# Graph layer and attention layer on one core: projections as three float32r products instead of seven block products in float32

## The chip, the cores and the metric

The kernel runs on one core of a Trainium2 chip. The metric is device time in microseconds of the whole program, as the median of three runs. A core has these engines: TensorE (PE in the profile, PEld for its weight loads), VectorE (DVE), ScalarE (ACT), GpSimd (POOL) and SyncE (SP, which here only issues DMAs). Each takes its instructions in order, and they wait for each other through semaphores. DMAs are issued from the queue of an engine; an issue that must wait for a buffer keeps what stands behind it waiting too.

## What is computed

The input x holds 64 elements of 256 rows and 512 columns; adj is a symmetric 256 x 256 graph of zeros and ones. Two layers follow each other, each with a residual and a normalisation of the rows. Cut to what matters:

```python
# layer 0
mi = x @ Wi.T                                  # Wi, Wj: 512 x 512
mj = x @ Wj.T
out0 = deg * (mi + b) + adj @ mj
h = layernorm(x + out0)
# layer 1, 8 heads of 64
q, k, v = h @ Wq.T + bq, h @ Wk.T + bk, h @ Wv.T + bv
scores = where(adj == 0, -inf, q @ k.T / 8)    # per head
attn = softmax(scores)
ao = attn @ v
y = layernorm(h + ao @ Wo.T + bo)
```

All is float32. The projections are those with Wq, Wk, Wv and Wo.

## The kernel before, in words

The main program, `unshifted_path`, works on pairs of elements: 32 groups of two (`NB = 2`, `NG = 32`). `for g in range(NG - 1)` is the main loop. A pass of it holds the attention of group g, layer 0 of group g + 1, the output projection of group g and the q, k and v projections of group g + 1; the first group's layer 0 and projections stand ahead of the loop (the prologue), the last group's attention after it.

Layer 0 of an element is a Strassen-like scheme (`l0_steps`): seven block products `step1` to `step7` of two matmuls each, 128 x 128 by 128 x 512, plain float32 (tiles `po`, weights `w0`, sums of x in `xS` from `sum_x`). Banks are called x, w, y and z; partial results are `u1`, `u2`, `u3` (tag `lu`). The result for the neighbours, `mj`, is cut into `hi` and `lo`, both float32r, and `neighbours` multiplies them with the graph: eight float32r matmuls of 512 columns (tile `pa`). `take` adds that to the residual `xh` and forms statistics, `give` normalises. x comes in twice, as `xh` (rows) and, in 32-row blocks, as `xB`, which DVE's 32 x 32 transposition turns into `xT` (`turn_x`). h goes to DRAM and back the same way (`send_h`, tiles `h_cols` and `hB`), and DVE turns it (`turn_h`).

The projections are a Strassen-Winograd scheme over the pair of elements (`pair_steps`, `qkv_steps`, `o_steps`): a projection is seven block products, each of four matmuls of 256 columns, float32 (tile `st`). Their left sides are blocks of h or of the attention output and sums of such blocks (`hS`, `oS`, made by `left_steps` on DVE); their right sides are seven `factor` tiles of 256 KB a projection, three of them blocks of the weights and four of them sums (`make_factors`, once, in the prologue), loaded from DRAM for every group through a ring of nine buffers (`stream`, `bring`), on SP's queue.

Attention goes in eight steps w a group, two heads a step, two steps a slot. `scores` makes a score tile `ps` (two banks); DVE adds the mask (`pe`), ACT takes the exponential, POOL adds the two halves (`pk`). `values` multiplies with v (`pav`), and `divide_two` has ACT copy that to `aoT`, TensorE make the denominators (`den`), DVE invert them (`rden`) and DMAs spread the inverses over partitions (`spread`); `multiply` applies them on POOL. POOL also sums the inverses in `rtot`, for a check at the end.

The order on the engines is written by hand for matmuls and for whatever passes through `in_order`; other instructions are placed by the scheduler. The score tiles have two buffers of two banks (`ps_s`), values one bank (`ps_v`), everything else three banks (`ps_m`).

Of the kernel before, what the change touches and what calls it, by code (L numbers as in the profile page):

```python
# [8 lines left out]
F32 = mybir.dt.float32  # L9
# [215 lines left out]
def unshifted_path(ctx, tc, flag, x, adj, wiT, wjT, b0, wqT, bq, wkT, bk, wvT, bv, woT, bo, out):  # L225
# [27 lines left out]
    AHEAD = 8  # L253
# [6 lines left out]
    p4 = ctx.enter_context(tc.tile_pool(name="p4", bufs=4))  # L260
    p6 = ctx.enter_context(tc.tile_pool(name="p6", bufs=6))
    stream = ctx.enter_context(tc.tile_pool(name="stream", bufs=AHEAD + 1))
# [35 lines left out]
    def load_x(b):  # L298
        if b < B:
            xh[b] = p6.tile([P, NT, D], F32, tag="xh", name="xh")  # L300
            nc.sync.dma_start(out=xh[b], in_=x[b].rearrange("(t p) d -> p t d", p=P))

    b_bc = p4.tile([P, D], F32, tag="u", name="b_bc")
    xB, hB = {}, {}

    def load_xB(b):
        if b < B:
            xB[b] = p1.tile([P, N // R, P], F32, tag="xB", name="xB")
            for q in range(D // P):
                nc.sync.dma_start(out=xB[b][q * R:(q + 1) * R],  # L310
                                  in_=x[b][:, q * P:(q + 1) * P].rearrange("(r a) n -> r a n", r=R))

# [11 lines left out]
    xT, xS, hT, hS, qT, kT, vv, aoT, oS = ({} for _ in range(9))  # L324


    ident = const.tile([P, P], F32, name="ident")
# [6 lines left out]
    rtot = const.tile([P, N], F32, name="rtot")  # L334
    nc.gpsimd.memset(rtot, 0.0)
# [7 lines left out]
    aT = p3.tile([P, NT, N], F32, tag="pk", name="aT")  # L343
    deg = small.tile([P, NT], F32, tag="deg", name="deg")
# [16 lines left out]
    def check_graph():  # L361


        exact = p1.tile([P, NT, N], F32, tag="oS", name="exact")
        in_order(nc.vector.tensor_tensor(exact, aT, graph.bitcast(F32), ALU.not_equal))
        in_order(nc.vector.tensor_reduce(inexact, exact.rearrange("p t n -> p (t n)"), AX.X, ALU.max))
        in_order(nc.vector.tensor_scalar(maskT, aT, 0.0, MASK, ALU.is_equal, ALU.mult))
# [9 lines left out]
    def load_bias(b, name):  # L377
        t = const.tile([P, NC], F32, tag=name, name=name)
        nc.sync.dma_start(out=t, in_=b)
        d = const.tile([P, 2], F32, tag=name + "d", name=name + "d")  # L380
        return t, d

    bq_sb, bqd = load_bias(bq, "bq")
    bk_sb, bkd = load_bias(bk, "bk")

    def bias_steps():
        for t, d in ((bq_sb, bqd), (bk_sb, bkd)):
            in_order(nc.vector.tensor_sub(d, t[:, 2:4], t[:, 0:2]))

    bv_t = small.tile([P, NC], F32, tag="bvt", name="bv_t")  # L390
    with nc.allow_non_contiguous_dma(reason="512 numbers, once"):
        nc.sync.dma_start(out=bv_t, in_=bv.rearrange("r (c p) -> p (r c)", p=P))
# [3 lines left out]
    def blocks_of(w):  # L396
        return (w.rearrange("(h c p) (j o) -> p h c j o", h=2, p=P, j=2) if w is woT else
                w.rearrange("(p h c) (j o) -> p h c j o", h=2, p=P, j=2))

    sources = {}  # L400
    for name, w in (("wq", wqT), ("wk", wkT), ("wv", wvT), ("wo", woT)):
        src = blocks_of(w)
        sources[name] = {B11: src[:, 0, :, 0], B21: src[:, 1, :, 0], B22: src[:, 1, :, 1]}


    def load_raw(w, tag):
        raw = p1.tile([P, 2, 2, 2, H], F32, tag=tag, name="raw")
        nc.sync.dma_start(out=raw.rearrange("p h c j o -> p (h c) (j o)"),
                          in_=w.rearrange("(c p) o -> p c o" if w is woT else "(p c) o -> p c o", p=P))
        return raw  # L410

    def make_factors(w, name, raw):
        kept = dram.tile([4, P, 2, H], F32, tag=name, name=name)
        t1, t2, t3, t4 = (p4.tile([P, 2, H], F32, tag="u", name="t") for _ in range(4))
        b11, b12, b21, b22 = (raw[:, h, :, j, :] for h in range(2) for j in range(2))
        for n, (t, p, m) in enumerate(((t1, b12, b11), (t2, b22, t1), (t3, b22, b12), (t4, b21, t2))):
            in_order(nc.vector.tensor_sub(t, p, m))
            nc.sync.dma_start(out=kept[n], in_=t)
        sources[name].update({T1: kept[0], T2: kept[1], T3: kept[2], T4: kept[3]})

    spread = p3.tile([P, NC, P], F32, tag="pk", name="spread")
# [3 lines left out]

    def fold_value_bias(raw):

        pb = score_bank("pb")
        for c in range(NC):
            h, kc = divmod(c, 2)  # L430
            matmul(pb, spread[:, c], raw[:, h, kc].rearrange("p j o -> p (j o)"),
                   start=(c == 0), stop=(c == NC - 1))
        nc.vector.tensor_add(bo_bc, pb, bo_bc)
# [4 lines left out]
    def bring():  # L438
        if queue:
            name, n = queue.pop(0)  # L440
            f = stream.tile([P, 2, H], F32, tag="factor", name="factor")
            nc.sync.dma_start(out=f, in_=sources[name][n])
            coming.append(f)

    def next_factor():
        f = coming.pop(0)
        bring()
        return f


    def norm_stats(t, order=anywhere):
# [3 lines left out]
        nc.vector.bn_aggr(mv, st)  # L455
        ve = small.tile([P, 1], F32, tag="ve", name="ve")
        nc.vector.tensor_scalar(ve, mv[:, 1:2], EPS, None, ALU.add)
# [3 lines left out]
        nc.gpsimd.tensor_tensor(rstd, ve, mhalf, ALU.pow)  # L461
# [26 lines left out]
    def turn_x(b, tag="xT"):  # L488
        if b < B:
            xT[b] = p1.tile([P, NC, N], F32, tag=tag, name="xT")  # L490
            transposed(xT[b], xB.pop(b))
            load_xB(b + 1)
# [9 lines left out]
    def l0_steps(b, late=False):  # L502
        banks, k = {}, {}
        order = in_order if late else anywhere
# [19 lines left out]
        def split(t):  # L524
            nc.scalar.copy(k["hi"][:, t, :], k["mj"][:, t, :])
            nc.gpsimd.tensor_tensor(k["lo"][:, t, :], k["mj"][:, t, :], k["hi"][:, t, :].bitcast(F32),
                                    ALU.subtract)

        def step1():
            product("x", raw(0, 0), B11, True)  # L530
            nc.scalar.copy(keeper("u1"), banks["x"])

        def step2():
            product("w", raw(1, 1), T4, True)
            add_scaled(1, banks["w"])

        def step3():
            product("x", raw(0, 1), B21, False)
            add_scaled(0, banks["x"])

        def step4():
            product("y", xS[b]["S2"], T2, True)
            nc.vector.tensor_add(keeper("u2"), banks["y"], k["u1"])

        def step5():
            product("z", xS[b]["S1"], T1, True)
            k["mj"] = p1.tile([P, NT, D], F32, tag="mj", name="mj")
            nc.vector.tensor_copy(k["mj"][:, 1, :], banks["z"])

        def step6():  # L550
            product("y", xS[b]["S3"], T3, False)
            nc.vector.tensor_add(keeper("u3"), banks["y"], k["u1"])
            nc.gpsimd.tensor_tensor(k["mj"][:, 1, :], k["mj"][:, 1, :], k["u3"], ALU.add)

            k["hi"] = p1.tile([P, NT, D], F32R, tag="hi", name="hi")
            k["lo"] = p1.tile([P, NT, D], F32R, tag="lo", name="lo")
            split(1)
            if not late:
                add_scaled(1, k["u3"])

        def step7():
            product("z", xS[b]["S4"], B22, False)
            order(nc.vector.tensor_add(k["mj"][:, 0, :], banks["z"], k["u2"]))
            split(0)
# [3 lines left out]
        def neighbours():  # L568
            k["pa"] = score_banks("pa")
            for i in (1, 0):  # L570
                for n, (j, part) in enumerate((j, part) for j in (1, 0) for part in ("hi", "lo")):
# [3 lines left out]
        def take(t):  # L575
            r = xh[b][:, t, :]
            if late and t == 1:
                in_order(add_scaled(1, k["u3"]))
            in_order(nc.vector.tensor_add(r, k["pa"][:, t, :], r))
            stats[t] = norm_stats(r, in_order)  # L580

        def give(t):
# [3 lines left out]
        return [step1, step2, step3, step4, step5, step6, step7, neighbours, lambda: take(1), lambda: take(0),  # L586
                lambda: give(1), lambda: send_h(b, 1), lambda: give(0), lambda: send_h(b, 0)]
# [530 lines left out]
```

## Time and profile before

| | us |
|---|---|
| median of three runs | 3068.26 |
| lowest and highest | 3067.78, 3070.22 |
| the profiled execution's own time | 3068.79 |
| its span, first to last instruction | 3066.9 |

The profile is of one execution. Rows give a line of the kernel, an engine, an operation, the tiles as out<-in, the shape and the count, then the busy time and the mean length of one in ns. Matmuls overlap, and their ends are modelled, so the step from one start to the next is a better measure than the length. A float32 matmul leaves two records, a float32r matmul one. A few groups of operations that the text uses:

| operation | engine | mean ns of one |
|---|---|---|
| mask addition `pe<-ps,maskT` | DVE | 1195 |
| reciprocal `rden<-den` | DVE | 1752 |
| row statistics `st<-xh` | DVE | 688 |
| transposition `hT<-hB`, 1024 elements | DVE | 2163 |
| exponential `pe<-pe` | ACT | 1058 |
| cast `hi<-mj` | ACT | 617 |
| sum of halves `pk<-pe` | POOL | 1278 |
| multiplication `aoT<-aoT,spread` | POOL | 1279 |
| bias addition `xh<-xh,degb`, 1024 elements | POOL | 2385 |

### The profile page before, as it was taken

The numbers are of one execution on the slowest core, as the hardware profiler recorded it, in microseconds if no ns is written. First come the engines' busy times: TensorE is split into PE (matmuls) and PEld (weight loads), VectorE is DVE, ScalarE is ACT, GpSimd is POOL, SyncE is SP. The second block draws the span as 40 slices with busy tenths as digits, with TensorE's granted clock in tenths as the row PEclk, the third lists the DMA queues.
The fourth block names the chain that finished last, engine by engine and source line by source line (L and its number), as shares of the span: only waits on it lengthen the run. The fifth ranks groups of instructions, "written<-read, shape, count | busy, mean of one in ns | idle before, by whom it ended". The sixth has DMA issues, their size and how long they took to land. (4 is left out here: it accounts for less than half of the span.)

```text
span 3066.9 us, 46810 instructions
## 1 busy us (share of the span) xinstructions
PE 3036.6 (99%) x16646; PEld 2124.6 (69%) x16646; DVE 2178.3 (71%) x3298; ACT 974.1 (32%) x1861; POOL 1519.5 (50%) x1255
## 2 busy tenths in 40 slices
PE   7999999999999999999999999999999999999998
PEld 4667766677766777666776667776677766677665
DVE  6776677766777667777677777677766777767775
ACT  2323333323333333332233332333333333323332
POOL 2544545544545445464454554454544546445453
PEclk9999999999999999999999999999999999999999
DMA  7455544455444555345553445544455444555333
GB/s 255 123 151 159 169 121 136 132 161 166 144 125 127 159 170 155 116 133 154 161 168 119 126 145 160 167 134 134 127 158 170 151 121 128 159 161 166 120 111 96
DMA packets 410411, 447.54 MB, mean 146 GB/s; under 512 B 40896, under 2 KB 300224, under 8 KB 409792
## 3 DMA queue, kind: packets, MB, share of 16 engines
q1 hardware_dynamic: 410176, 444.50, 48.8%
q8 instruction: 136, 2.23, 0.3%
q14 instruction: 99, 0.81, 0.1%
HBM read 340.79 MB, written 70.25 MB: 134 GB/s over the span
## 5 line engine op out<-in xcount | busy, mean ns | idle before, releaser
L461 POOL TENSOR_TENSOR rstd<-ve,mhalf 128x1 f32<-128x1 f32 x256 | 140.5, 552 | 707.3 <-DVE below L459 707.3
L816 POOL TENSOR_TENSOR pk<-pe 128x512 f32<-128x512 f32 x256 | 323.1, 1278 | 322.2 <-ACT pe L813 322.2
L290 PE MATMUL po<-w,xS 128*128 128x512 f32 x1024 | 462.2, 599 | 0.7 <-DVE xS L478 0.7
L290 PE MATMUL st<-hS,factor 128*128 128x256 f32 x2048 | 453.2, 379 | 1.5 <-DVE u L689 1.2
L290 PEld LDWEIGHTS st<-hS,factor 128*128 128x128 f32 x2048 | 388.4, 190 | 56.3 <-DVE xh L744 1.7
L813 ACT ACTIVATE pe<-pe 128x1024 f32<-128x1024 f32 x256 | 270.8, 1058 | 364.4 <-DVE pe L809 364.4
L290 PE MATMUL po<-w,xT 128*128 128x512 f32 x768 | 352.1, 601 | 14.8 <-DVE xS L477 9.3
L290 PE MATMUL st<-hT,factor 128*128 128x256 f32 x1536 | 352.5, 379 | 0.7 <-ACT hT L626 0.7
L290 PEld LDWEIGHTS po<-w,xS 128*128 128x128 f32 x1024 | 189.6, 190 | 235.6 <-issue 206.3
L809 DVE TENSOR_TENSOR pe<-ps,maskT 128x1024 f32<-128x1024 f32 x256 | 298.0, 1195 | 35.4 <-PE ps L290 35.4
L290 PEld LDWEIGHTS st<-hT,factor 128*128 128x128 f32 x1536 | 291.9, 190 | 41.8 <-ACT hT L626 0.9
L886 DVE RECIPROCAL rden<-den 128x256 f32<-128x256 f32 x127 | 222.5, 1752 | 76.6 <-PE den L290 73.6
L290 PEld LDWEIGHTS po<-w,xT 128*128 128x128 f32 x768 | 144.2, 191 | 181.9 <-issue 162.8
L887 POOL TENSOR_TENSOR rtot<-rtot,rden 128x256 f32<-128x256 f32 x127 | 106.8, 841 | 320.1 <-DVE rden L886 320.1
L290 PE MATMUL ps<-qT,kT 64*128 64x256 f32 x2048 | 265.0, 393 | 0.0
L290 PE MATMUL pav<-pe,v_sb 128*32 128x256 f32 x4096 | 248.4, 382 | 1.9 <-ACT pe L813 1.9
L290 PEld LDWEIGHTS ps<-qT,kT 64*128 64x128 f32 x2048 | 184.5, 186 | 78.1 <-issue 38.6
L744 DVE TENSOR_TENSOR xh<-st,xh 128x512 f32<-128x512 f32 x186 | 144.5, 777 | 132.2 <-PE st L290 132.2
L290 PE MATMUL st<-factor,hS 128*128 128x256 f32 x1024 | 234.8, 382 | 0.0
L290 PEld LDWEIGHTS pav<-pe,v_sb 128*32 128x32 f32 x4096 | 119.8, 110 | 164.3 <-issue 95.4
L290 PE MATMUL st<-factor,oS 128*128 128x256 f32 x992 | 224.2, 379 | 0.0
L290 PEld LDWEIGHTS st<-factor,hS 128*128 128x128 f32 x1024 | 192.1, 190 | 35.2 <-issue 10.6
(115 smaller groups left out, 4648.2 us busy)
## 6 DMA issues: line engine op xcount, KB each, us to landing
xB<-in_x_dram SPq DMA_DIRECT2D x256, 128.0 KB, 3.9
xh<-in_x_dram SPq DMA_DIRECT2D x64, 512.0 KB, 4.2
factor<-wq SPq DMA_DIRECT2D x128, 256.0 KB, 4.2
factor<-wk SPq DMA_DIRECT2D x128, 256.0 KB, 2.8
factor<-wv SPq DMA_DIRECT2D x128, 256.0 KB, 2.6
spread<-rden SPq DMA_DIRECT2D x1016, 32.0 KB, 1.9
factor<-wo SPq DMA_DIRECT2D x124, 256.0 KB, 3.2
h_cols<-xh SPq DMA_DIRECT2D x124, 256.0 KB, 3.0
```

Of the source, the lines that this page charges most:

```text
L290: in_order(nc.tensor.matmul(*args, **kw))
L461: nc.gpsimd.tensor_tensor(rstd, ve, mhalf, ALU.pow)
L744: nc.vector.tensor_add(dst, src, dst)
L809: nc.vector.tensor_add(pe.rearrange("p j t q -> p j (t q)"), ps.rearrange("p j t q -> p j (t q)"), maskT.rearrange("p t q -> p (t q)").uns ...
L813: in_order(nc.scalar.activation(flat, flat, AF.Exp, scale=QSCALE, accum_out=etot[:, NB * g + i, pr:pr + 1]))
L816: nc.gpsimd.tensor_tensor(pk, pe[:, :, 0, :], pe[:, :, 1, :], ALU.add)
L886: nc.vector.reciprocal(rden, den)
L887: nc.gpsimd.tensor_tensor(rtot, rtot, rden, ALU.add)
```

## The change

The projections no longer use block products. Each operand is cut into a head and a low part, and a product takes three float32r passes: head by head, low part by lifted low part, and a difference by a difference, which are added up in two banks X and Y; the result is X times a constant plus Y. h becomes the three tiles `hA` (head), `hL` (low) and `hD` (difference), the attention output likewise in the buffers of q, k and v. Each weight tile has three planes, made in the prologue by `make` on ACT and DVE and kept in DRAM; a factor is now 768 KB, there are 16 a group (four a projection), in a ring of six, and they are loaded from ACT's queue.

With this come other edits: the sums `hS` and `oS` go; the `lo` part of `mj` moves from POOL to DVE; the sum of inverses moves from POOL's `rtot` addition to an accumulating copy on ACT; the pairing of partitions in `values` and `den` is changed so that inverses are spread by four DMAs of 64 partitions instead of eight of 32; layer 0 of the next group starts earlier (`step1` to `step4` of its first element run in the pass before); h is sent, fetched and turned in halves of 128 rows, the first element's in the fourth slot and beside the output projection; nearly every instruction is put in program order; `xh` has five buffers instead of six; the fold of v's bias into the output bias moves into the first pass of the loop.

```diff
-    AHEAD = 8
+    RING = 6
+    UP, DOWN, LIFT = 1 + 2.0 ** -12, 1 - 2.0 ** -13, 2.0 ** 12
...
-    p6 = ctx.enter_context(tc.tile_pool(name="p6", bufs=6))
-    stream = ctx.enter_context(tc.tile_pool(name="stream", bufs=AHEAD + 1))
+    p5 = ctx.enter_context(tc.tile_pool(name="p5", bufs=5))
+    stream = ctx.enter_context(tc.tile_pool(name="stream", bufs=RING))
...
     def bring():
         if queue:
-            name, n = queue.pop(0)
-            f = stream.tile([P, 2, H], F32, tag="factor", name="factor")
-            nc.sync.dma_start(out=f, in_=sources[name][n])
+            name, j, first = queue.pop(0)
+            f = stream.tile([P, 3, D], F32R, tag="factor", name="factor")
+            if first:
+                make(f, name, j)
+            else:
+                in_order(nc.scalar.dma_start(out=f.bitcast(F32), in_=kept[name][j]))
             coming.append(f)
...
+    def make(f, name, j):
+        head, lift, diff = (f[:, i, :].rearrange("p (c o) -> p c o", c=NC) for i in range(3))
+        low = p3.tile([P, NC, P], F32, tag="lu", name="low")
+        for cs, raw in pieces(name, j):
+            in_order(nc.scalar.activation(head[:, cs], raw, AF.Identity, scale=DOWN))
+            in_order(nc.vector.tensor_sub(low[:, cs], raw, head[:, cs].bitcast(F32)))
+            in_order(nc.scalar.activation(lift[:, cs], low[:, cs], AF.Identity, scale=LIFT))
+        in_order(nc.vector.scalar_tensor_tensor(diff, low, LIFT, head.bitcast(F32), ALU.mult, ALU.subtract))
+        nc.sync.dma_start(out=kept[name][j], in_=f.bitcast(F32))
...
-            nc.gpsimd.tensor_tensor(k["lo"][:, t, :], k["mj"][:, t, :], k["hi"][:, t, :].bitcast(F32),
-                                    ALU.subtract)
+        def lows(t):
+            in_order(nc.vector.tensor_tensor(k["lo"][:, t, :], k["mj"][:, t, :], k["hi"][:, t, :].bitcast(F32),
+                                             ALU.subtract))
...
+    def split_head(parts, src):
+        in_order(nc.scalar.activation(parts[0], src, AF.Identity, scale=DOWN))
+
+    def split_diff(parts, src):
+        in_order(nc.vector.scalar_tensor_tensor(parts[2], parts[0].bitcast(F32), UP, src, ALU.mult, ALU.subtract))
+
+    def split_low(parts, src, engine):
+        in_order(engine.tensor_tensor(parts[1], src, parts[0].bitcast(F32), ALU.subtract))
...
+    def cols_product(banks, parts, f):
+        X, Y = banks
+        head, low, diff = parts
+        f = f.rearrange("p k (c o) -> p k c o", c=NC)
+        for c in range(NC):
+            matmul(X, f[:, 0, c, :], head[:, c, :], start=(c == 0), stop=False, skip_group_check=True)
+        for c in range(NC):
+            matmul(Y, f[:, 2, c, :], diff[:, c, :], start=(c == 0), stop=(c == NC - 1), skip_group_check=True)
+        for c in range(NC):
+            matmul(X, f[:, 1, c, :], low[:, c, :], start=False, stop=(c == NC - 1), skip_group_check=True)
+
+    def qk_step(g, store, tag, bias, m, kind):
+        def run():
+            if m == 0:
+                store[g] = p1.tile([P, NC, NB * N], F32, tag=tag, name=tag)
+            X, Y = banks = pair(kind)
+            cols_product(banks, hP[g], coming.pop(0))
+            dst = store[g][:, m, :]
+            in_order(nc.scalar.activation(dst, X, AF.Identity, bias=bias[:, m:m + 1], scale=UP))
+            bring()
+            in_order(nc.vector.tensor_add(dst, Y, dst))
+        return run
...
-        nc.gpsimd.tensor_tensor(rtot, rtot, rden, ALU.add)
...
+        spread = p1.tile([P, 2, N], F32, tag="spread", name="spread")
+        for half in range(2):
+            for pp in range(2):
+                issuer = nc.scalar if last and pp else nc.sync
+                in_order(issuer.dma_start(out=spread[half * DH:(half + 1) * DH, pp, :],
+                                          in_=rden[pp * DH:(pp + 1) * DH, :]))
+        total(rden, total_out)
         products.append((dst, spread))
```

`v_pair` makes v for one element (24 matmuls, four factors shared by both halves of its rows), and `o_steps` has three parts: `one(0)` and `one(1)` for the first element's halves, `two` for the second element, in which the second element's h is turned as well. The last two slots and the projections of the loop now read:

```diff
+        values(g, 4)
+        values(g, 5)
+        multiply()
+        h11 = turn_h(b1, 1)
+        split_head(*h11)
+        split_low(*h11, nc.gpsimd)
+        divide_two(g, 5)
+        load_xB(b3 + 1)
+        now, later = scores(g, 6), scores(g, 7)
+        now()
+        low2()
+        head, diff = three(("qT", "kT"))
+        split_head([head[:, :, :N]], aoT[g][:, :, :N])
+        later()
+        split_diff(*h11)
+        if g + 2 < NG:
+            next_p[0][1]()
+        split_diff([head[:, :, :N], None, diff[:, :, :N]], aoT[g][:, :, :N])
+        nb2()
+        add2(1)
+        add2(0)
+        multiply()
+        aoP[g] = [head, None, diff]
+        split_head(*ao_parts(g, 1, upper))
+
+        values(g, 6)
+        values(g, 7)
+        aoP[g][1], = three(("v",))
+        split_low(*ao_parts(g, 0, every), nc.gpsimd)
+        stat2(1)
+        divide_two(g, 7)
+        split_low(*ao_parts(g, 1, upper), nc.gpsimd)
+        split_diff(*ao_parts(g, 1, upper))
+        if g + 2 < NG:
+            next_p[0][2]()
+        give2(1)
+        send_h(b2, 1)
+        stat2(0)
+        give2(0)
+        fetch_h(b2, 1)
+        send_h(b2, 0)
+        multiply()
+        h10 = turn_h(b1, 0)
+        split_head(*h10)
+        split_head(*ao_parts(g, 1, lower))
+        split_low(*ao_parts(g, 1, lower), nc.gpsimd)
+        split_low(*h10, nc.gpsimd)
+        fetch_h(b2, 0)
+        p, q = next_p, next_q
+        v, q_, k = projection_steps(g + 1)
+        end = finish_steps(g)
+        o = o_steps(g, "SMAS", lambda t: turn_h(b2, t))
+        o[0]()
+        split_diff(*h10)
+        split_diff(*ao_parts(g, 1, lower))
+        o[1]()
+        run([o[2], v[0]])
+        sum_x(b3)
+        v[1]()
+        turn_x(b3 + 1)
+        run([end[0], q_[0], end[1], k[0], end[2], q_[1], end[3], k[1]])
```

## Prediction

> **What bounds the kernel now.** I read the page's busy shares first, then the matmul timeline of one group of two batch elements, then busy times by stage, then single rows.
>
> ```profile
> PE 3036.6 (99%) x16646; PEld 2124.6 (69%) x16646; DVE 2178.3 (71%) x3298; ACT 974.1 (32%) x1861; POOL 1519.5 (50%) x1255
> ```
>
> PE has no idle time to give, so only its own work counts, until another engine is late. In the timeline (start, us, engine, line, out<-in) one group runs from one `st<-factor,aoT` to the next:
>
> ```profile
> 1555.32 1.99 PE L290 MATMUL st<-factor,aoT 128*128 128x256 f32 x8
> ...
> 1557.61 0.40 PE L290 MATMUL pa<-hi,graph 128*128 128x512 f32 x1
> ...
> 1558.78 0.40 PE L290 MATMUL pa<-lo,graph 128*128 128x512 f32 x1
> ...
> 1562.47 5.34 PE L290 MATMUL st<-hT,factor 128*128 128x256 f32 x24
> 1567.65 1.89 PE L290 MATMUL st<-factor,aoT 128*128 128x256 f32 x8
> ...
> 1649.71 1.99 PE L290 MATMUL st<-factor,aoT 128*128 128x256 f32 x8
> ```
>
> A period is 1649.71 - 1555.32 = 94.39 us; there are 31. A plain float32 record of 256 columns takes (1567.65 - 1562.47)/24 = 0.216 us, and a matmul is two records. The only float32r matmuls, `pa`, step by (1558.78 - 1557.61)/5 = 0.234 us at 512 columns, one record each.
>
> ```profile
> 1513.40:1555.30 41.90, 41.90 (x273) 20.79 (x271) 31.09 (x39) 14.23 (x26) 24.35 (x21) 1.00 0.24 69
> 1555.30:1607.80 52.50, 52.50 (x253) 45.60 (x250) 36.24 (x64) 16.10 (x33) 23.15 (x20) 1.00 0.70 206
> sum 94.40, PE 94.40 PEld 66.39 DVE 67.34 ACT 30.33 POOL 47.50; mean PE 47.20 PEld 33.20 DVE 33.67 ACT 15.17 POOL 23.75
> ```
>
> These are the attention stage and the projection stage. DVE has 67.3 us of work in 94.4, so it has room, but two rows show that it isn't free to use it:
>
> ```profile
> 1531.69 0.42 DVE L479 TENSOR_TENSOR xS<-xT 128x256 f32<-128x256 f32 x1
> 1532.03 1.50 DVE L480 TENSOR_TENSOR xS<-xT,xS 128x256 f32<-128x256 f32 x1
> ...
> 1531.76 2.90 POOL L526 TENSOR_TENSOR lo<-mj,hi 128x512 fp32r<-128x512 f32 x2 [0.73 <-ACT hi L525]
> ```
>
> The same subtraction takes 0.42 us, and 1.50 us beside a POOL operation.
>
> **What the Trainium skill says.** "FP8 and Floating Point Precision", TensorE Precision Notes: true float32 is four passes through the array. The trace agrees (512 columns as two records of 0.43 us). "TensorE: Matmul & The Clock Gate", Back-to-back issue gap: N/2.4 + 2.5 ns, 216 ns for 512 columns; the plain records agree, the float32r ones show 234, and the measurement decides. "SBUF — State Buffer", SBUF: two separate sides: DVE and GpSimd share a port pair under an exclusive lock, which a DVE operation with two SBUF inputs takes against a GpSimd operation that reads SBUF; the loser waits for the whole instruction. The 1.50 us row agrees.
>
> **The change part by part.**
>
> *Products.* Out go 4 projections x 7 products x 4 matmuls x 2 records = 224 records x 0.216 = 48.4 us a group. In come 4 x 16 x 3 = 192 float32r matmuls of 512 columns x 0.234 = 44.9. PE's floor falls by 3.5, to 90.9. Their cost isn't shown for weights that change at every matmul and for two banks in turn: 0.216 (the skill's gap) would give 3.4 more, 0.25 (as far above the measured value) would take 3.2. I take 0.234, whose weight loads are also repeated.
>
> *DVE.* Out: sums hS, oS (8 x 0.69), combination of q, k, v (10 x 0.69, 4 x 0.48), o (5 x 0.69, 1.22), copies mj (2 x 0.69), two 2.1 us turns: 24.6 us. In: Y added to q, k, v (12 x 0.69), X and Y of o (4 x 0.75, 4 x 0.69), four half turns (half of 2.1, an estimate), differences of h and ao (6 x 0.69, 1.2), lows of mj, formerly POOL's (4 x 0.69), mj (2 x 0.69): 27.8. So 70.5 us.
>
> *ACT* gains heads (7, at 0.62 like the cast `hi`, one double), totals of inverses (4 x 0.5) and 18 DMA issues, about +7 to 37 us. *POOL* loses `rtot`, `lo`, `mj` and the additions of u (18.9) and gains lows (10): 38.6 us.
>
> *Where DVE is late.* DVE now stands in program order almost throughout. From the second element's second product (w, `q[1]`) to the second v pair (`v[1]`), PE has 4 attention slots x 4.23 (1520.32 to 1524.55 in the timeline), 8 layer-0 products x 1.72, two `pa` x 1.87, 72 projection matmuls x 0.234 and some 0.5 of switching: 51.7 us. DVE has 6 mask additions x 1.15, 4 reciprocals x 1.68, 4 statistics x 1.08, one turn of 2.07, four of 1.06, 8.1 of layer-0 additions, 2.6 of neighbour additions, 1.95 of lows, 1.7 of x sums, 5.05 of differences and 5.4 of o: 47.0. Then `v[1]` needs the last h difference and the bank that o's last addition frees. Room: 4.5 us after 0.2 for the hand-over. POOL works 25 of these 51.7 us, and DVE has twelve places with two SBUF inputs. Laying both orders side by side I find waits of 1.2 (u3 scaled, behind pk 5), 1.2 (low of mj, behind a multiplication), 0.75 (difference of h, behind pk 6), 1.2 (difference of ao, behind pk 7), 0.4 and 1.0 (upper and lower ao differences, behind their lows), 0.5 and 0.8 (last two h differences), and 0.75 where a difference waits for ACT's head: 7.8 us. The added waits hold what follows them: behind the lower ao difference stand o's additions, two turns, and so `v[1]`. 7.8 - 4.5 = 3.3 us late. Bounds: 0 (no collision beyond the room) and about 7 (each collides at a full 1.28 us, 15 less the 4.5, less what PE's own waits for the exponentials cover). I take 3.3.
>
> *Late next.* In q and k each product's Y bank must be freed by ACT within the four X matmuls, 0.93 us. With normalisations in between I find slack of 0.1 to 0.4 us, and book 0.2. So stalls of 3.5 return what PE gained: period 94.4.
>
> *h through DRAM.* Halves of 256 KB, four sends and four fetches, on SP in order; a fetch waits 3.0 us for its send. The last half lands about 1 to 3 us before its turn. Nothing is booked; if late, it delays `v[1]` one for one. SP loses 28 factor issues and 18 of 32 spreads; factors go to ACT's queue, where each stands behind the eviction that frees it. `load_x` waits there for a store (five buffers, not six); the additions behind it have until the next group.
>
> *Bytes.* Factors go from 28 x 256 KB to 16 x 768 KB, and a group from 14.0 to 19.4 MB. q1 moved 444.5 MB in 48.8% of the span, 297 GB/s while busy: 65 us of 94, with six factors in the ring. Hidden.
>
> *Prologue.* All 16 factors are made by ACT (head), DVE (low), ACT (lift) in ACT's order, 0.62 + 0.69 + 0.62 plus hand-overs, 2.2 to 2.6 us each, some 38 us of ACT's time that the old weight sums, on DVE, didn't need. Before, products begin at 48.07 and the loop at 96.57. After, ACT has from 48 on 38 of making, 15 of evictions, norms and heads, 5 of waiting for the graph check on DVE; then 14 us of PE stand behind the last made factor: the loop begins near 120. Four products (6.9) are then done that were inside the loop, so compare with 103.5: +17. The bias fold (3.4) moves into the loop, +3.4. Together +21, bounds 8 and 30.
>
> *Sum.* 3066.9 + 21 + 31 x (94.4 - 94.39) = 3088 us of span. The profiled run took 3068.79 around its 3066.9, and the median is 3068.26: forecast 3090.
>
> **Rivals.** (a) Forecast: DVE's port waits eat PE's gain, 3075 to 3130. Chance 0.42. (b) Faster: the waits stay within the 4.5 us of room, because POOL has 9 us less to do and each blocked operation also spaces the next; stalls are about 1.3, period 92.2, 3090 - 31 x 2.2 = 3022. It decides at a period of 93.7, 21/31 = 0.7 below the present one: 2.8 us of stall. For it: in the present order PE shows almost no idle time although DVE meets the same lock; against it: DVE has 3 us more to do, in a fixed order. 0.38. (c) DVE is the bound from slot two on, collisions near the full price: period 97, 3171. 0.11. (d) Factor transfers arrive late, since 12.6 MB are wanted mostly in q and k: 2 us for each of the last three, 3090 + 31 x 6 = 3276. Against it: 206 GB/s now in that stage. 0.02. (e) Between, within 0.2% of before. 0.07. That it doesn't do what it says is out: in the changed program's order each projection has 4 x 12 such matmuls.
>
> **Chances.** 0.2% is about what this measurement can tell from no change. Slower 0.42 + 0.11 + 0.02 = 0.55, same 0.07, faster 0.38. Range: (b) spreads over 2975 to 3060 with the float32r bounds, (c) to 3220; leaving a tenth on each side, 2998 to 3180; the forecast's own is 3075 to 3130.
>
> **What would show it.** Right: float32r steps of 0.234; the loop beginning near 120; PE idle before `v[1]` and in the second o stage, ended by DVE; DVE rows of 512 elements stretched from 0.65 to 1.3 and more beside POOL; DVE above 75%. Wrong: periods near 92 (b), waits for `factor` DMAs (d), steps of 0.216.

## The result and the profile after

| | before | after |
|---|---|---|
| median of four runs (lowest to highest), us | 3069.24 (3067.78 to 3070.41) | 3344.83 (3342.89 to 3354.18) |
| profiled execution, us | 3068.79 | 3342.89 |
| its span, us | 3066.9 | 3341.1 |
| median period of a group, us | 94.39 | 102.37 |
| mean TensorE clock granted | 0.999 | 0.949 |

The time is 1.0904 times that of before (95% interval 1.0883 to 1.0925). The forecast of 3090 had the direction right; the size is far off, and 3344.83 lies above the range of 2998 to 3180. By the starts of the output projection's first matmul in the 31 passes of the loop, the 274.2 us of longer span are 30.2 ahead of the first output projection, 239.4 in the 30 periods after it (7.98 each) and 4.7 behind the last. So the question is the period.

The page of after: the busy shares, then two DMA queues (packets, MB, share of 16 engines). q10 is the queue of ACT with the factors, q1 that of SP.

```profile
PE 3000.3 (90%) x15638; PEld 1954.2 (58%) x15638; DVE 2365.8 (71%) x3477; ACT 1186.9 (36%) x2247; POOL 1335.9 (40%) x992
...
q10 hardware_dynamic: 75808, 391.02, 33.0%
q1 hardware_dynamic: 229584, 215.69, 21.7%
```

PE was 99% busy before and is 90% now. DVE is at 71% in both, so a bound by DVE's amount of work is out. The DMA engines are at 55% on average, which hides a stretch that turns out to matter.

A v pair is the 24 matmuls that make v for one element. PE's timeline of after around the change from the first v pair to the second (start, us, engine, line, tiles; in brackets the idle time ahead and who ended it):

```profile
1517.77 0.40 PE L290 MATMUL pxy<-factor,hL 128*128 128x512 f32 x1
1526.99 0.77 PE L290 MATMUL pxy<-factor,hA 128*128 128x512 f32 x1 [8.82 <-DVE xh L743]
1527.56 0.63 PE L290 MATMUL pxy<-factor,hD 128*128 128x512 f32 x1
...
1531.83 0.44 PE L290 MATMUL px<-factor,hL 128*128 128x512 f32 x1
1532.10 0.40 PE L290 MATMUL pxy<-factor,hA 128*128 128x512 f32 x1
```

Nearly all the lost time is in this one place, once a group: 8.73 us of idle time on average over the groups, and then matmuls that step by 0.43 us instead of 0.227. The 12 steps from 1526.99 to 1532.10 take 5.11 us where 2.72 would do, 2.4 more. With 0.56 us before a `factor,kT` matmul of the output projection and 0.21 before `factor,v`, that is 11.9 us a group. PE's own work is 90.3 us (it is measured below), and 90.3 + 11.9 = 102.2, where the period is 102.4.

The bracket names DVE's addition at L743, the second of the additions that put the output projection into `xh`. It is easy to stop here and blame DVE, as the prediction did. DVE's own timeline of after shows what DVE did before that addition:

```profile
1509.87 0.69 DVE L743 TENSOR_TENSOR xh<-py,xh 128x512 f32<-128x512 f32 x1
1513.67 1.12 DVE L496 STREAM_TRANSPOSE hF<-hB 128x512 f32<-128x512 f32 x1 [3.11 <-DMA hB<-h_cols]
1515.48 0.69 DVE L605 SCALAR_TENSOR_TENSOR hD<-hA,hF 128x512 fp32r<-128x512 f32 x1 [0.70 <-ACT hA L602]
1521.85 1.12 DVE L496 STREAM_TRANSPOSE hF<-hB 128x512 f32<-128x512 f32 x1 [5.67 <-DMA hB<-h_cols]
...
1524.14 1.38 DVE L605 SCALAR_TENSOR_TENSOR hD<-hA,hF 128x512 fp32r<-128x512 f32 x1
1525.44 0.68 DVE L739 SCALAR_TENSOR_TENSOR xh<-pxy,xh 128x512 f32<-128x512 f32 x1
1526.16 0.69 DVE L743 TENSOR_TENSOR xh<-pxy,xh 128x512 f32<-128x512 f32 x1
```

At 1510.5 DVE had nothing left that it could do; PE started the first v pair only at 1512.38. So DVE was 1.9 us ahead, and then it stood twice, 3.11 and 5.67 us, for the two halves of h to come back from DRAM (2.1 and 5.9 in the median of the groups). The last half landed 1521.85 - 1517.77 = 4.1 us after PE's last matmul had started. Another 5.0 us passed between that landing and the end of the addition at 1526.85, because DVE then has the transposition, two additions, the difference of this half and two more additions to do, in this order. 4.1 + 5.0 = 9.1 of the 9.2 us between the starts of the two matmuls. In these 5.0 us the difference of h takes 1.38 us, where the row of the other half takes 0.69: POOL works on the low part of the same half at that time, so some 0.7 us of the waits that the prediction counted do lie on the path.

Why did the half land so late? The timeline of after shows the DMA issues on SP's queue (L624 sends, L629 fetches):

```profile
1506.17 0.36 SPq L624 DMA_DIRECT2D h_cols<-xh  x1
1508.57 0.34 SPq L629 DMA_DIRECT2D hB<-h_cols  x1
1509.00 0.39 SPq L624 DMA_DIRECT2D h_cols<-xh  x1
1516.48 0.33 SPq L629 DMA_DIRECT2D hB<-h_cols  x1
```

ACT's queue of after, over the same time:

```profile
1508.22 1.69 ACTq L441 DMA_DIRECT2D factor<-wv  x2
...
1514.88 0.33 ACTq L441 DMA_DIRECT2D factor<-wq  x1
1515.30 0.39 ACTq L441 DMA_DIRECT2D factor<-wk  x1
```

The first send took 2.4 us (its fetch could be issued at 1508.57). The second took 1516.48 - 1509.00 = 7.5, and its fetch 1521.85 - 1516.48 = 5.4. In the median of the groups it is the same: 7.5 and 5.4 us. Beside them run four factor loads of 768 KB, which the output projection's third part releases as it uses up its own factors. The order on SP may have a share too: the second half of h was ready when ACT had normalised it, but its send stands behind the first half's fetch and went out 1.5 us later (median). No run puts both sends ahead of both fetches, so what that alone is worth is not known.

The windows of after, for the 14 us in which these transfers meet and the 8 us behind them (span of the window, its length, then the busy time of PE, PEld, DVE, ACT and POOL, and at the end the clock, the DMA engines' busy share and GB/s):

```profile
1508.00:1522.00 14.00, 10.17 (x43) 7.54 (x41) 4.48 (x7) 1.12 (x2) 4.85 (x3) 0.99 0.80 281
1522.00:1530.00 8.00, 3.01 (x7) 2.46 (x8) 7.40 (x12) 1.60 (x3) 1.26 (x1) 0.50 0.00 0
```

For 14 us the DMA engines move 281 GB/s at a busy share of 0.80. That is near the 297 GB/s that SP's queue reached while busy in the kernel before, but it is no ceiling: from 1517 to 1520, between the second send and the arrival of the last half, the same trace has 410 GB/s at a busy share of 1.0, nearly all of it factors. For the next 8 us the engines move nothing. An average over the group hides both. The two lines also show the clock: 0.99 in the first window, 0.50 in the second.

### The profile page after: what moved, and what is told of

It reads as the page before. It is cut to its first block, busy times and chain, and to the rows that moved or that the text cites. A ratio compares the mean times of both kernels' runs of the same rounds, so it can differ in the third digit from the quotient of the medians.

```text
span 3341.1 us, 42660 instructions
## 1 busy us (share of the span) xinstructions
PE 3000.3 (90%) x15638; PEld 1954.2 (58%) x15638; DVE 2365.8 (71%) x3477; ACT 1186.9 (36%) x2247; POOL 1335.9 (40%) x992
## 3 DMA queue, kind: packets, MB, share of 16 engines
q1 hardware_dynamic: 229584, 215.69, 21.7%
## 5 line engine op out<-in xcount | busy, mean ns | idle before, releaser
L290 PE MATMUL po<-w,xT 128*128 128x512 f32 x768 | 376.3, 613 | 13.5 <-DVE xS L488 8.4
L290 PE MATMUL pxy<-factor,hA 128*128 128x512 f32 x256 | 119.4, 466 | 272.1 <-DVE xh L743 269.0
L608 POOL TENSOR_TENSOR hL<-hF,hA 128x512 fp32r<-128x512 f32 x124 | 186.8, 1507 | 425.9 <-ACT hA L602 425.9
L496 DVE STREAM_TRANSPOSE hF<-hB 128x512 f32<-128x512 f32 x124 | 141.1, 1138 | 251.5 <-DMA hB<-h_cols 251.5
L373 POOL TENSOR_TENSOR xh<-xh,degb 128x1024 f32<-128x1024 f32 x64 | 152.5, 2383 | 291.2 <-issue 80.7
L697 DVE TENSOR_TENSOR kT<-py,kT 128x512 f32<-128x512 f32 x128 | 88.5, 691 | 253.1 <-ACT kT L695 253.1
L602 ACT ACTIVATE hA<-hF 128x512 fp32r<-128x512 f32 x124 | 77.7, 627 | 457.4 <-DVE hF L496 457.4
L290 PEld LDWEIGHTS pxy<-factor,hA 128*128 128x128 f32 x256 | 56.0, 219 | 296.7 <-issue 281.2
L478 ACT ACTIVATE xh<-xh,shift,rstd 128x512 f32<-128x512 f32 x256 | 208.8, 816 | 8.6
L854 POOL TENSOR_TENSOR aoT<-aoT,spread 128x512 f32<-128x512 f32 x127 | 206.1, 1623 | 11.7 <-DMA spread<-rden 10.6
```

What stands on the lines that cost most here:

```text
L290: in_order(nc.tensor.matmul(*args, **kw))
L373: in_order(nc.gpsimd.tensor_tensor(xh[b], xh[b], degb, ALU.add))
L478: order(nc.scalar.activation(t, t, AF.Identity, bias=shift, scale=rstd))
L496: in_order(nc.vector.transpose(dst.rearrange("p c (n a) -> p a c n", n=R), blocks.rearrange("p a (r c) -> p a c r", c=NC)))
L608: in_order(engine.tensor_tensor(parts[1], src, parts[0].bitcast(F32), ALU.subtract))
L697: in_order(nc.vector.tensor_add(dst, Y, dst))
```

## The experiments

Theory after the profile of the change (called the transfer theory): the halves of h are late because 768 KB loads share the DMA engines with them. Rivals: DVE is late, by waits at the port or by its order, as the prediction had it; or the clock's fall is the main cost. Eight kernels were run; all are versions of the changed kernel, and none leaves out a part of the computation.

**Filling the gap with matmuls.** The first v pair, which needs only the first element's h, is computed twice.

```diff
-            for c in range(NC):
+            for c in (range(NC) if last else [*range(NC), *range(NC)]):
```

> The first v pair's 24 matmuls run twice (the second time over the first, same result): 24 x 0.227 = 5.4 us of matmuls more in each of 31 groups. Theory of transfers (the second element's h halves come late, whatever TensorE does): the second v pair starts no later than now, the wait before it shrinks from 8.8 to about 3.3 us, the clock is not taken down, so the 12 matmuls behind the wait step by 0.227 instead of 0.43: 2.4 us a group less, about 3345 - 31 x 2.4 = 3270. Theory that VectorE is late because it follows TensorE: the wait moves with the extra work, 5.4 us a group more, 3510. If the slow matmuls behind the wait have another cause than the wait: unchanged, 3345.

Measured: 3316.09 us (3314.63 to 3320.97), 1.0805 of before (1.0787 to 1.0823), mean clock 0.983. PE's timeline of this kernel:

```profile
1510.16 0.47 PE L290 MATMUL pxy<-factor,hA 128*128 128x512 f32 x1 [2.72 <-DVE xh L743]
...
1511.70 0.63 PE L290 MATMUL pxy<-factor,hA 128*128 128x512 f32 x1
1512.13 0.63 PE L290 MATMUL pxy<-factor,hD 128*128 128x512 f32 x1
```

Twenty-four more matmuls a group, 5.4 us, cost nothing: the idle time fell from 8.73 to 3.24 us. So what PE waits for does not come later when PE has more to do. The gain, 29 us or 0.9 a group, is less than the 2.4 that slowed matmuls cost in the changed kernel, and the time lies 46 us above the forecast. The lines show why: after an idle time of only 2.72 us the step still rises to 0.43, 1.5 us later. Of 30 groups, 21 had such slow matmuls (1.7 us lost, in the median) and 9, with idle times of 2.0 to 3.3 us, lost 0.1.

The idle time alone does not tell the two kinds apart, but the trace's record of the granted clock does. The clock changes only at multiples of 3.41 us from its first change, in every run here. In the loop of this kernel it fell after each of the 21 stretches between two such moments in which PE had been busy for 0.40 of the time or less, and after none with 0.48 or more. So an idle time of 2.7 us that falls into one stretch costs the clock, and one of 3.3 us that two stretches share does not; and since the fall comes at the end of the stretch, PE may be at work again by then. The rival that the clock is the main cost does not fit: by the steps it takes 2.4 of the 11.9 us lost in the changed kernel.

**Factor loads behind the last half of h.** The output projection's third part keeps its four factors and asks for the next four only after ACT has taken the head of the last half.

```diff
-                        rows_of_product(banks[t], parts, NT + t, coming[0], c, which)
-                coming.pop(0)
-                bring()
+                        rows_of_product(banks[t], parts, NT + t, coming[c], c, which)
...
             h0 = turn(0)
             split_head(*h0)
+            for _ in range(NC):
+                coming.pop(0)
+                bring()
```

> The four factor loads that are issued within o's third part (two of wv, one of wq, one of wk) are issued only after the last half of h has been turned. Theory of transfers: the sends and fetches of the second element's h no longer share the DMA engines with 768 KB loads; the second send takes 2.3 us instead of 7.4 and the fetches 2.5 to 3 instead of 5; the last turn on VectorE starts about 6 us earlier. TensorE then waits in the first v pair for wv instead, for some 4 us: period 97 to 99, 3180 to 3240. Theory of VectorE's ports: the sends and fetches hardly change, the last turn moves by under 1 us, and the wait for wv comes on top: slower, above 3400.

Measured: 3234.36 us (3231.45 to 3237.53), 1.054 (1.0522 to 1.0558), period 98.89. First SP's issues in this kernel's timeline:

```profile
1559.57 0.39 SPq L624 DMA_DIRECT2D h_cols<-xh  x1
1562.82 0.33 SPq L629 DMA_DIRECT2D hB<-h_cols  x1
```

Then DVE's timeline of the same kernel, at the last transposition, which waits 1.00 us and not 5.67:

```profile
1565.54 1.14 DVE L496 STREAM_TRANSPOSE hF<-hB 128x512 f32<-128x512 f32 x1 [1.00 <-DMA hB<-h_cols]
```

And PE's, in the first v pair:

```profile
1570.97 0.79 PE L290 MATMUL px<-factor,hA 128*128 128x512 f32 x1 [4.83 <-DMA factor<-wv]
```

The second send now takes 3.3 us and its fetch 2.7, 6.0 together instead of 12.9, with the same instructions and the same bytes; only what stands beside them differs. That is the transfer theory's cause, shown by taking it away. The 110 us that it gives are not the whole price, since the wait has changed its name: PE now stands 4.65 us a group for the third factor of v, which was asked for at 1566.8, and the clock falls in this gap too.

**VectorE's order.** In the changed kernel the additions stand behind the transposition that waits. Here they go ahead of it.

```diff
             split_diff(*h1)
-            h0 = turn(0)
-            split_head(*h0)
-            split_low(*h0, nc.gpsimd)
             add_x(1, 0, banks[0])
             add_y(1, 0, banks[0])
-            split_diff(*h0)
             add_x(1, 1, banks[1])
             add_y(1, 1, banks[1])
+            h0 = turn(0)
+            split_head(*h0)
+            split_low(*h0, nc.gpsimd)
+            split_diff(*h0)
```

> The changed kernel with the four additions of the output projection's third part put ahead of the transposition of the last half of h in VectorE's order; nothing else. In the changed kernel they stand behind it, and the first matmul of the second v pair waits for the last of them, since it frees its bank. Transfer theory (the last half of h is late itself): the wait moves by a few matmuls, from the first to the fourth, which is the first to read that half, and VectorE has less to do after the landing, some 2 us: between 0 and 2.5 us a group less, 3265 to 3345. Rival (the wait is the place of the additions in VectorE's order, and h alone would be in time): most of the 8.7 us and of the slowed matmuls after it go, 10 us a group, 3035 to 3080.

Measured: 3252.91 us (3247.57 to 3256.62), 1.0597 (1.0579 to 1.0614), period 99.26. PE's timeline of this kernel:

```profile
1578.45 0.47 PE L290 MATMUL pxy<-factor,hA 128*128 128x512 f32 x1 [0.41 <-DVE xh L743]
...
1583.56 0.80 PE L290 MATMUL px<-factor,hA 128*128 128x512 f32 x1 [4.17 <-ACT hA L602]
```

DVE's, at the last transposition:

```profile
1581.72 1.13 DVE L496 STREAM_TRANSPOSE hF<-hB 128x512 f32<-128x512 f32 x1 [3.41 <-DMA hB<-h_cols]
```

The wait moved from the first to the fourth matmul, as the transfer theory said, but the time lies in neither band: the gain, 3.1 us a group, is above that theory's 2.5 and far below the rival's 10. After the landing 1.8 us pass until PE goes on (1581.72 to 1583.56), where in the changed kernel it was 5.0. So the order in DVE's list is a second cause, in series with the first. Taken away alone, it leaves more than half of the lost time.

**More work for VectorE.** The transposition of the first element's second half is made three times, 2.2 us more for DVE in the stretch in which the prediction had it late.

```diff
+        twice = hB[b1, 0]
         h10 = turn_h(b1, 0)
+        transposed(h10[1], twice)
+        transposed(h10[1], twice)
```

> The changed kernel with the transposition of the first element's second half made three times instead of once, directly after one another in the fourth slot: 2 x 1.1 = 2.2 us more of VectorE's time a group, inside the stretch in which the prediction had VectorE late. Transfer theory (VectorE had finished its list 1.9 us before TensorE ended the output projection and then waited for the halves of h): the wait before the first v pair stays set by the DMA, so between 0 and 0.5 us a group, 3345 to 3360, and the idle time of TensorE before that pair stays between 8 and 9 us. Prediction's theory (VectorE late through waits at the port, each further microsecond of its work delays the v pair one for one): 2.2 x 31 = 68 us more, 3413.

Measured: 3319.16 us (3317.22 to 3326.42), 1.0821 (1.0803 to 1.0839). PE's timeline of this kernel:

```profile
1510.52 0.50 PE L290 MATMUL py<-factor,kT 128*128 128x512 f32 x1 [1.84 <-DVE kT L605]
...
1525.12 0.77 PE L290 MATMUL pxy<-factor,hA 128*128 128x512 f32 x1 [6.33 <-DVE xh L743]
```

DVE's, with the transposition made three times and the one that waits:

```profile
1503.49 3.44 DVE L496 STREAM_TRANSPOSE hF<-hB 128x512 f32<-128x512 f32 x3
...
1519.97 1.12 DVE L496 STREAM_TRANSPOSE hF<-hB 128x512 f32<-128x512 f32 x1 [5.76 <-DMA hB<-h_cols]
```

(The wait that the expectation places before the first v pair is the one before the second.) More work made the kernel 26 us faster; both theories missed that, the DVE theory by 94 us. DVE's delay does reach PE, but earlier, in the output projection (1.85 us a group before `factor,kT` and 0.7 before `factor,qT`, instead of 0.56 together), and the later wait shrinks by more than that: the sum of the idle times is 8.5 us, after 9.5. In most groups PE only waits earlier and not longer, for the last half of h comes when it came before. Counted from the first matmul of the output projection, it lands after 21.7 us in the changed kernel, 21.7 with the gap filled, 21.6 with the additions first and 21.6 here, but after 14.6 with the factor loads moved (medians of the traces). Neither PE's work nor DVE's order or work moves it; the loads do. Most periods stay at 102.3; six fall to between 95 and just over 100, and in these six the last half lands after 17.7 to 20.3 us. That the small wait in the output projection spreads the factor loads there is an inference; it was not tried by itself.

**TensorE turns the second element's h.** Eight transpositions of 128 x 128 by TensorE, in the middle of the output projection's third part, replace two sends, two fetches and two of DVE's transpositions. The score tile that they write is used up by the first v pair. The low parts of this h are now made by DVE instead of POOL, and all of its cutting stands ahead of the additions, so both causes are taken away at once here.

```diff
-        send_h(b2, 1)
...
-        fetch_h(b2, 1)
-        send_h(b2, 0)
...
-        fetch_h(b2, 0)
...
+        both = score_banks("pt_h")
...
+        pts = {t: both[:, 1 - t, :].rearrange("p (c n) -> p c n", c=NC) for t in (1, 0)}
+        for t in (1, 0):
+            for c in range(NC):
+                transpose(pts[t][:, c, :], xh[b][:, t, :].rearrange("p (n c) -> p c n", c=NC)[:, c, :], ident)
+        for t in (1, 0):
...
+            split_three(cut_parts(hP[g], slice(0, NC), cols), pts[t], nc.vector)
```

> The second element's h is turned by TensorE (8 transpositions, about 1 us a group) into a free pair of banks within o's third part and cut from there; it no longer goes through DRAM. The first element's still does. Theory of transfers: the wait before the second v pair goes (8.7 us) and with it the slow clock (2.5 us), TensorE pays 1 us: period 102.4 - 10 = 92 to 93, total 3030 to 3060, under the kernel before. Theory of VectorE's ports: VectorE has two turns of 1.1 us less, but its port waits stay, so 3 us or more of wait before the second v pair remain: period 95 or more, 3115 or more.

Measured: 3042.21 us (3041.34 to 3042.62), 0.991 of before (0.9893 to 0.9926), period 92.63, clock 0.995. The busy shares on the page of this kernel:

```profile
PE 2961.1 (97%) x15886; PEld 1942.7 (64%) x15886; DVE 2311.2 (76%) x3477; ACT 1192.1 (39%) x2247; POOL 1238.1 (41%) x930
```

Its timeline of PE, from the transpositions to the bank that they used:

```profile
1569.03 1.12 PE L293 MATMUL pt_h<-ident,xh 128*128 128x128 f32 x8
1569.91 0.47 PE L290 MATMUL px<-factor,qT 128*128 128x512 f32 x1
...
1574.12 0.50 PE L290 MATMUL pt_h<-factor,hA 128*128 128x512 f32 x1 [0.55 <-DVE hL L608]
```

The eight transpositions cost PE 0.88 us, and the period is 9.7 us shorter. The second v pair has no wait any more, the clock no longer falls in the loop, and the change, with this one trip to DRAM taken out, is 0.9% faster than the kernel before. DVE is busy almost without a break from the fourth slot to the second v pair, with the same stretched rows beside POOL, and all that PE waits for it is the 0.85 us of the next experiment.

**The first v pair's order.** What was left was 0.85 us a group before the first matmul into the bank that had held the turned h. The next kernel takes one half of the rows first, so that this bank is needed later.

```diff
-            for c in range(NC):
-                for t in (1, 0):
+            for c, t in ([(c, t) for c in range(NC) for t in (1, 0)] if last
+                         else [(c, t) for t in (1, 0) for c in range(NC)]):
```

> The kernel in which TensorE turns the second element's h, with one more edit: the first v pair takes its 12 matmuls for one half of the rows and then the 12 for the other, instead of the two halves in turn, so that the bank which the turning used is needed after 12 matmuls (2.7 us) and not after 3. If the 0.85 us a group before that bank's first matmul is a wait for VectorE's reading of the turned h alone: all of it goes, 31 x 0.85 = 26 us less, 3016. If VectorE is late there as a whole (it is busy almost without a break from the fourth slot on), the wait moves to the second v pair's bank, and half of it or less goes: 3029 to 3042.

Measured: 3039.65 us (3036.05 to 3042.18), 0.9901 (0.9885 to 0.9918). That is 2.6 us below the run before, whose runs lie within 1.3 us and this kernel's within 6.1: no clear difference. It is in the band of the second expectation, but not by its reason. PE's timeline of this kernel:

```profile
1572.42 0.39 PE L290 MATMUL px<-factor,hL 128*128 128x512 f32 x1
1573.54 0.50 PE L290 MATMUL px<-factor,hA 128*128 128x512 f32 x1 [0.73 <-DMA factor<-wv]
```

The wait for DVE is gone, and a wait for the fourth factor, which this order needs after 9 matmuls, is there with the same 0.85 us on average.

**Making weight tiles one ahead.** In the prologue ACT made a head, waited for DVE's low part, and made the lifted low part. Now the next head is issued in between.

```diff
+            if first:
+                finish = make(f, name, j)
+            while pending:
+                pending.pop()()
+            if first:
+                pending.append(finish)
...
+        def finish():
+            for cs, _ in cuts:
+                in_order(nc.scalar.activation(lift[:, cs], low[:, cs], AF.Identity, scale=LIFT))
+            in_order(nc.vector.scalar_tensor_tensor(diff, low, LIFT, head.bitcast(F32), ALU.mult, ALU.subtract))
+            nc.sync.dma_start(out=kept[name][j], in_=f.bitcast(F32))
```

> As the run before, and in the prologue the head of the next weight tile is issued on ScalarE ahead of the lifted low part of the present one, so that ScalarE does not stand idle 0.76 us for VectorE between the two. If the making of the 16 tiles by ScalarE sets the prologue, as the prediction has it, some 0.76 us for each of the first six and a part of the later ten go: the loop begins 4 to 8 us before 122.7, and the time falls by as much. If the raw weights or TensorE's own waits for banks set it: less than 1 us.

Measured: 3031.31 us (3029.23 to 3031.87), 0.9875 (0.9859 to 0.9892), 8.3 us less than the run before. The loop's first work, the fold of v's bias, starts at 112.03 us, where it was 123.70: 11.7 us earlier, more than the 4 to 8 expected, of which the time keeps 8.3. So ACT's order set a part of the prologue.

**Both waits of the first v pair at once.** Three factors with one half of the rows, the same three with the other half, then the fourth with both.

```diff
-                         else [(c, t) for t in (1, 0) for c in range(NC)]):
+                         else [(c, t) for cs in ((0, 1, 2), (3,)) for t in (1, 0) for c in cs]):
```

> As the run before, but the first v pair takes its matmuls in another order: three weight tiles with one half of the rows, the same three with the other half, then the fourth tile with both. The bank that held the turned h is then needed after 9 matmuls (2.0 us) instead of 3 or 12, the fourth weight tile after 18 (4.1 us) instead of 9. If the 0.85 us a group of both earlier orders were two separate waits of that size, one for VectorE's reading of the bank and one for the landing of the fourth tile, both are covered: 31 x 0.85 = 26 us less, 3005. If VectorE or the transfers are late as a whole, the wait turns up again further on (the second v pair), and the time stays between 3020 and 3032.

Measured: 2996.11 us (2994.09 to 2997.27), 0.9757 of before (0.9744 to 0.977), 35 us less than the run before; period 91.41. The busy shares on the page of this kernel:

```profile
PE 2945.1 (98%) x15886; PEld 1941.8 (65%) x15886; DVE 2318.2 (77%) x3477; ACT 1190.5 (40%) x2247; POOL 1242.0 (41%) x930
```

PE's timeline, where the first matmul into that bank follows without a wait:

```profile
1544.80 0.39 PE L290 MATMUL px<-factor,hL 128*128 128x512 f32 x1
1545.02 0.39 PE L290 MATMUL pt_h<-factor,hA 128*128 128x512 f32 x1
```

The two waits were separate and both are covered. They account for some 26 us, as forecast; where the other 9 come from was not tried. A typical period now has 0.2 us of idle time, so PE's own work for a group is 91.41 - 0.19 - 0.88 of transpositions = 90.3 us. This version is 2.4% faster than the kernel before and 10.4% faster than the change as it was made.

## Why the prediction was wrong

- *Products*: right in the main. The float32r matmuls step by 0.227 us with weights that change each time. With 192 of them that is 1.3 us less than at the 0.234 taken, and would make the floor 89.6 us; it measured 90.3, and where the other 0.7 goes was not looked for. PE's gain of about 4 us a group (94.4 to 90.3) is real, as the last experiment shows.
- *Where DVE is late*: the place, `v[1]`, is right, and so is the name in the bracket; the cause is not. The step also has a slip in its sum: the DVE terms that it lists add up to 49.05 us, not 47.0. With 49.05 the room is 2.45 us instead of 4.5, DVE comes 5.35 late, and the same working gives 3154: nearer to the result, by the wrong mechanism. In the trace DVE had finished its list 1.9 us before PE began the first v pair. The collisions that the step counted are there (the fourth slot's rows of 1.52, 1.75, 1.48 and 1.92 us, against 0.74, 0.7, 0.7 and 1.2 unhindered, 3.3 us in all, and 0.7 in the difference behind the landing), but fewer than the 7.8 booked, and 2.2 us more of DVE's work did not lengthen the period.
- *h through DRAM*: this is the step that failed. "The last half lands about 1 to 3 us before its turn. Nothing is booked; if late, it delays `v[1]` one for one." It landed 4.1 us after PE's last matmul had started. The 3.0 us for a send are those of the kernel before, whose factor loads are of 256 KB; here, beside loads of 768 KB, the second send took 7.5 us, and the fetch behind it 5.4. "One for one" was too little as well: behind the landing stand 5.0 us of DVE's list, since its order puts the output projection's additions behind the waiting transposition. The prediction asked what stands behind a waiting DVE instruction for its port waits, but not for this DMA wait.
- *Bytes*: "65 of 94 us", "Hidden". The bytes were right and the average was the wrong thing to ask. Four loads and three transfers of h, 4 x 768 + 3 x 256 KB = 3.9 MB, all fall between 1508.2 and 1521.9 us; at the prediction's own 297 GB/s that is 13.2 us of transfers, and 13.7 were seen. That the two agree so closely is luck, since the engines were busy for 0.80 of the time and moved 410 GB/s where they were full; at that rate the same bytes take 9.6 us. The sum could have been made from the diff: the third part of the output projection pops four factors, and each pop issues a load while h is on its way.
- *Late next*: the q and k products cost PE no idle time worth naming. The booked 0.2 us is not seen there; 0.56 us stood in the output projection instead.
- *Prologue*: the loop's begin is right, 122.8 us against the 120 forecast, with the fold's 3.4 us behind it; the term is too small. At the first output projection the kernel is 30.2 us later than the one before, and 4.7 more come after the last, where 21 were booked in all. The step took off 6.9 us for four products done early, but the first pass makes three of the next group's four ahead of its output projection, so 1.7 us come back there; and the last pass, which has none to make, has 3.4 us of other waits. The term is 14 of the 255 us missed.
- Not in the prediction at all: the clock that falls in the gap and costs 2.4 us a group more.
- Rival (d), at a chance of 0.02, looked at the transfers, but had the factors late in q and k. In the changed kernel PE waits for factors 0.03 us a group; they made h late instead. Rival (b)'s period of 92.2 was what the change could reach once that trip to DRAM was gone (92.6, then 91.4).

In the sum, the term of 94.4 should have been 90.3 + 4.1 (landing) + 5.0 (DVE's list behind it) - 0.1 (the last matmul's own 0.23, which lies in the 4.1, less the 0.14 of hand-over to PE) + 2.4 (clock) + 0.8 (output projection) = 102.5, against 102.4 measured.

## What to carry to other kernels

When a small transfer has a deadline, add up the bytes that are issued between its issue and its deadline, not those of the whole period: a dense burst followed by nothing looks like a half idle queue in every average. Then ask what stands behind the instruction that waits for the landing, for its list comes on top of the delay. The engine that a wait's bracket names may only be the last in a chain; read its own idle time before giving it the blame.

## What the runs showed of the hardware

- TensorE's clock falls in a gap, to 0.50 in the window shown. After 8.8 us of idle time the next 12 matmuls stepped by 0.43 us instead of 0.227. After gaps of 2.7 to 5 us the same was seen in most groups, partly with a delay of up to 1.5 us after the restart; in 9 groups of one kernel, with gaps of 2.0 to 3.3 us, it wasn't. In the clock records the changes lie 3.41 us or multiples of it apart. With the gap filled it fell after stretches of 3.41 us with 0.40 of PE's busy time or less, and not after 0.48 or more; in the other runs the border lies somewhere from 0.4 to 0.6.
- A float32r matmul of 512 columns stepped by 0.227 us in runs of matmuls with new weights each time.
- A 256 KB send that took 2.3 us ahead of the 768 KB loads took 7.5 us beside those of another queue, and 3.2 us when these were moved away; the fetch behind it took 5.4 us, and 2.6 without them (medians over the groups).
- Eight 128 x 128 float32 transpositions by TensorE took 0.88 us in the midst of matmuls, against 6.0 us for one 256 KB half through DRAM, send and fetch, with no factor load beside it.
